# A hybrid layer on one core: attention stacks widened to 128 rows with zero rows, the first sequence's softplus in halves, idle identity products, and three weight loads moved

## Chip, core and metric

The kernel runs on one core of a Trainium2 chip. The metric is the time on the device in microseconds (us); the kernel before took 939.68 us, the median of three runs (939.14 to 942.08).

The core's engines are named as in the profile: PE is TensorE (PEld its weight loads), DVE VectorE, ACT ScalarE, POOL GpSimd, and SP the engine whose queue issues most transfers. A "q" behind an engine's name (SPq, ACTq, POOLq) is that engine issuing a DMA.

## What is computed

The input is x, 4 sequences of 512 tokens with 128 channels. Four blocks follow each other, each added to its input after a layer norm. Cut to the lines that matter here:

```python
x = x + attn_a(layernorm(x))     # rms norm, Mamba block, residual, rms norm, mixture of experts
x = x + ffn(layernorm(x))        # integer weights times 1/127: silu(x Wg) * (x Wu), then Wd
x = x + attn_b(layernorm(x))     # 16 heads of 8, causal softmax, low-rank keys and values
x = x + ffn(layernorm(x))        # the same weights again
# in the Mamba block, for each of 256 inner channels and 16 states:
delta = softplus(dbc[..., :64] @ dt_proj_w + dt_proj_b);  A = -exp(A_log)
h = exp(delta * A) * h + (delta * x) * B;  y = sum over states of h * C
# the mixture of experts: 8 experts, the best 2 for each token
```

## The kernel before, in words

Everything lives in one function, `block_kernel`, in two stages. All line numbers are those of the kernel before.

**Stage 1, the scans (up to about 405 us of the profile).** For each of the 4 sequences, `front` (L707) prepares the Mamba inputs and then 16 steps of `scan` (L860) run, one for each state, over tiles of 128 partitions x 1024 (two groups of 128 channels, 512 tokens each). A step has a fixed shape. ACT makes the decays `da` (L812). PE spreads a row of B over the partitions into `pb` (L822). DVE multiplies `bx = du * pb` (L854) and runs the recurrence `hst` (L874). POOL multiplies `hc = hst * cs` (L886), where `cs` is a row of C that SP fetches (L816) from DRAM, where L769 has put it. PE adds `hc` into `yp` with the identity matrix (L832). The tile `cs` has three buffers, `hst` two, and `bx` one (it fills the PSUM pool `ps_x`).

`front(0)` runs before the first scan, with nothing beside it: layer-norm statistics on DVE, `hn` (L710), a transpose by PE into `hT`, the convolution as 8 products `pm` (L723) with `w_k` as weights, `xi` (L729), the gate `sz` (L740), the scaled residual input `h0` (L743), `pdt` and its copy `dt` (L747, L752), B and C as `pbc` with `bc` and `bc_c` (L757 to L767), and the softplus (L777 to L801): `pd`, |.| and relu of it, exp(-|.|), ln(1 + .), and a correction of what adding 1 rounds off. Its result is `delta`; POOL multiplies it with `xi` to `du` (L803). For sequences 1 to 3 the same generator is drawn out over the steps of the sequence before it, a piece at every `yield`.

Other generators are drawn out beside the scans in the same way, as streams: `close` and `route` of a finished sequence, `scatter` of its tokens to their experts' rows, `experts` (tiles of 128 tokens: two products with 512 columns, a gate, a product back; 256 KB for each of three weight loads), `combine`, `first_ffn`, `project`. One of them is `early` (L661), which runs in the steps of sequence 0. It fills the experts' token buffers `xg` in DRAM with zeros, by 8 transfers of 1 MB on SP's queue (L680), from an SBUF tile with the tag "y". It then loads the three weights of the feed-forward blocks, one after the other, into a tile of the same tag (`raw`, L697), and DVE turns each into float (L693).

**What sets the order.** In stage 1 the order on PE, DVE, ACT and SP is the order of the program text (L34, `manual_schedule`), and each engine and each queue works through it strictly. POOL's multiplication of a step is made to wait for the last small DVE instruction that was drawn into the step (L892). The attention stage has no such order: there the framework's scheduler orders each engine by its own estimate, so that an edit can also move its neighbours.

**Stage 2, attention (to the end).** It works in 8 units of 8 heads. Queries and keys are held as three bf16 parts of their float values, stacked as 72 rows: 9 pairs of parts by 8 dimensions, in tiles `qs` and `ks` of 96 partitions, with 3 buffers each. `fill` (L1079) loads a unit by 6 transfers from DRAM. `maxima` (L1090) multiplies 72 rows of queries with 72 rows of keys (L1104), adds the causal mask by a product with the identity (L1108) and takes row maxima on DVE (L1100). The maxima go back as three more bf16 rows of `qs` (L1133, L1134), against three rows of -1 in `ks` (`below`, L1062). `exps` (L1140) multiplies the 75 rows the other way round (L1157), with a mask again (L1165), and ACT takes the exponential (L1170): 10 tiles for each group of four heads. `weigh` (L1173) multiplies with the values (L1184): four heads side by side, each with 32 columns of the array. Beside these run what is left of the experts' tiles, and the feed-forward blocks and projections of later sequences.

Of the kernel before, what the change touches and what calls it, by code (L numbers as in the profile page):

```python
# [8 lines left out]
F32 = mybir.dt.float32  # L9
# [7 lines left out]
P = 128  # L17
# [20 lines left out]
def block_kernel(ctx, tc, x, rms1_w, rms2_w, in_proj_w, conv_w, conv_b, x_proj_w,  # L38
# [51 lines left out]
    nc.gpsimd.memset(below, -1.0)  # L90
    identb = const.tile([P, P], BF16, tag="identb", name="identb")
# [80 lines left out]
    def transposed(ps, dst, src, scale=None):  # L172

        pt = ps.tile([P, L], F32, tag="mm" if ps is ps_m else "sc", name="pt")
        for t in range(NT):
            nc.tensor.transpose(pt[:, t * P : (t + 1) * P], src[:, t, :], ident)
        if scale is None:
            nc.scalar.copy(dst, pt)
        else:
            nc.scalar.activation(dst, pt, AF.Copy, scale=scale)  # L180
# [416 lines left out]
    with ExitStack() as first:  # L597
# [28 lines left out]
        w_o = load("w_o", [P, C], W_oT)  # L626
        hT = w1.tile([P, L + KW - 1], F32, tag="hT", name="hT")
# [33 lines left out]
        def early():  # L661

            for b in range(2, B):
# [23 lines left out]
            raw = None  # L687
            for dst, src in (
                (fwg, w_gateT), (fwu, w_upT), (fwd, w_downT.rearrange("(c p) m -> p c m", p=P)),
                (None, None),  # L690
            ):
                if raw is not None:
                    nc.vector.tensor_scalar(raw[0], raw[1], 1.0 / 127.0, None, ALU.mult)  # L693
                yield
                if dst is not None:
                    raw = dst, w1.tile(list(dst.shape), I32, tag="y", name="raw")
                    nc.sync.dma_start(raw[1], src)  # L697
# [8 lines left out]

        def front(b):  # L707
# [4 lines left out]
            transposed(ps_s, hT[:, KW - 1 :], hn, r1w[:, 0, :])  # L712
# [22 lines left out]
            for e in range(NE):  # L735
                pm = ps_s.tile([P, L], F32, tag="sc", name="pm")
                nc.tensor.matmul(
                    pm, w_in[:, EI + e * P : EI + (e + 1) * P], hT[:, KW - 1 :], start=True, stop=True
                )
                nc.scalar.activation(sz[b][:, e, :], pm, AF.Silu)  # L740
            yield
            h0[b] = w2.tile([P, NT, C], F32, tag="h0", name=f"h0_{b}")
            scaled(h0[b], xs[b], norms["r"][:, 0, b], norms["m"][:, 0, b])  # L743
            yield "sc"
# [7 lines left out]
            nc.scalar.copy(dt[b], pm[0:DTR, :])  # L752
            yield
# [15 lines left out]
            nc.sync.dma_start(c_d[b], cr[NS : 2 * NS, :])  # L769
            yield  # L770

# [574 lines left out]
```

## Time and profile before

| what | us |
|---|---|
| median of three runs | 939.68 |
| the profiled execution's own time | 941.45 |
| its span, from the first instruction to the last | 939.6 |
| PE busy (share of the span) | 734.1 (78%) |
| DVE busy | 580.3 (62%) |
| ACT busy | 411.2 (44%) |
| POOL busy | 309.4 (33%) |
| first scan step begins (DVE) | 44.61 |
| first attention product begins (PE) | 470.44 |
| mean granted PE clock, share of full speed | 0.854 |

The profile is of one execution; 1.85 us of its own time lie outside its span. "Busy" counts an engine's own instructions. Each view that is shown later gives, for an instruction or a group of instructions: when it starts, how long it takes, the engine, the line, the operation, what it writes from what it reads, and in brackets how long the engine had been idle before and what ended that. PE's records of float products come in pairs, so that one product of 128x512 counts as two. The page cuts the span into 40 slices of 23.5 us; a digit is a share in tenths.

### The profile page before, as it was taken

The page shows a single profiled execution, that of the slowest core. Times are in us where ns is not written, and L with a number is a line of the kernel's source. Part 1 is how long each engine was busy: PE and PEld are TensorE (multiplying, and loading weights), DVE is VectorE, ACT ScalarE, POOL GpSimd, SP SyncE. Part 2 cuts the span into 40 slices and gives each one's busy share as a digit, 9 for nine tenths or more (in the row PEclk, how much of TensorE's full clock was granted, in tenths as well). Part 3 has the DMA queues.
Part 4 walks back from the last instruction along what each step waited for, and adds up shares of the span by engine and source line. Part 5 has one row for each costly group of instructions (what it writes and reads, how often), then busy time and mean ns, then how long its engine had stood idle before and what let it go on. Part 6 is the DMA issues. An engine that isn't in the chain of part 4 may idle for free. (4 is left out here: it accounts for less than half of the span.)

```text
span 939.6 us, 11943 instructions
## 1 busy us (share of the span) xinstructions
PE 734.1 (78%) x3763; PEld 429.0 (46%) x3763; DVE 580.3 (62%) x1151; ACT 411.2 (44%) x794; POOL 309.4 (33%) x243
## 2 busy tenths in 40 slices
PE   5386698689879865788398799789858997889854
PEld 2132243255356621557357476458724454355432
DVE  4395999899989898747274552166544156566311
ACT  2836548535854431324103354503345533554641
POOL 1153664856556348432402104000161402300010
PEclk9688789789989977799759599979968897997987
DMA  4138221163157412516546235817410330600000
GB/s 103 35 140 325 65 68 47 53 194 112 64 171 233 132 46 82 172 46 202 178 125 204 80 117 168 211 45 220 143 43 3 93 87 7 163 16 3 3 12 11
DMA packets 84480, 99.16 MB, mean 106 GB/s; under 512 B 10370, under 2 KB 56458, under 8 KB 83242
## 3 DMA queue, kind: packets, MB, share of 16 engines
q1 hardware_dynamic: 78881, 87.09, 31.3%
q0 software_dynamic: 4352, 10.89, 3.6%
q10 hardware_dynamic: 1184, 0.43, 0.2%
q8 instruction: 30, 0.49, 0.2%
q14 instruction: 33, 0.26, 0.1%
HBM read 76.67 MB, written 21.63 MB: 105 GB/s over the span
## 5 line engine op out<-in xcount | busy, mean ns | idle before, releaser
L886 POOL TENSOR_TENSOR hc<-hst,cs 128x1024 f32<-128x1024 f32 x64 | 150.6, 2353 | 138.7 <-issue 34.3
L832 PE MATMUL yp<-hc,ident 128*128 128x512 f32 x256 | 150.6, 718 | 43.6 <-POOL hc L886 42.5
L874 DVE TENSOR_TENSOR_SCAN hst<-da,bx 128x1024 f32<-128x1024 f32 x64 | 146.3, 2286 | 10.7 <-POOL hc L886 3.7
L1100 DVE TENSOR_REDUCE mx<-sc 128x1 f32<-128x384 f32 (+3 forms) x168 | 102.7, 636 | 66.4 <-PE sc L1108 64.8
L832 PEld LDWEIGHTS yp<-hc,ident 128*128 128x128 f32 x256 | 52.7, 220 | 140.6 <-POOL hc L886 98.9
L1170 ACT ACTIVATE p<-st 128x512 f32<-128x512 f32 x160 | 90.9, 598 | 34.3 <-PE st L1165 31.0
L812 ACT ACTIVATE da<-delta,A 128x512 f32<-128x512 f32 (+1 forms) x128 | 84.7, 715 | 41.1 <-DVE hst L874 38.5
L1104 PE MATMUL sc<-ks,qs 72*128 72x128 bf16 (+3 forms) x256 | 76.7, 358 | 15.5 <-DMA ks<-k_d 8.2
L854 DVE TENSOR_TENSOR bx<-du,pb 128x1024 f32<-128x1024 f32 x64 | 78.3, 1223 | 5.0 <-POOL du L803 2.5
L319 DVE SCALAR_TENSOR_TENSOR thm<-thm,mpg 128x512 f32<-128x512 f32 x53 | 36.1, 680 | 70.4 <-ACT thm L380 70.4
L374 PE MATMUL mpg<-xTm,wgu 128*128 128x128 f32 x424 | 67.1, 301 | 11.1 <-DMA wgu<-in_Wg_dram 6.7
L1157 PE MATMUL st<-qs,ks 75*128 75x512 bf16 (+3 forms) x256 | 67.7, 331 | 10.3 <-ACT p L1170 5.6
L374 PEld LDWEIGHTS mpg<-xTm,wgu 128*128 128x128 f32 x424 | 60.3, 214 | 20.3 <-issue 8.4
L374 PE MATMUL mpu<-xTm,wgu 128*128 128x128 f32 x424 | 62.2, 292 | 5.8 <-DVE mh L320 4.1
L1133 POOL DMA_DIRECT2D m_d<-mT x8 | 4.4, 550 | 184.3 <-ACT mT L1131 184.3
L367 ACT ACTIVATE xTm<-mpt,r2w 128x128 f32<-128x128 f32 x53 | 19.4, 366 | 102.9 <-PE mpt L365 102.9
L386 PE MATMUL mpd<-wd,mh 128*128 128x128 f32 x424 | 60.2, 286 | 2.8 <-ACT xTm L367 2.3
L374 PEld LDWEIGHTS mpu<-xTm,wgu 128*128 128x128 f32 x424 | 57.3, 209 | 8.7 <-DVE mh L320 4.4
L822 PE MATMUL pb<-bc,pick 96*128 96x512 bf16 x64 | 27.4, 429 | 41.8 <-DVE bx L854 38.0
L386 PEld LDWEIGHTS mpd<-wd,mh 128*128 128x128 f32 x424 | 53.4, 197 | 7.0 <-ACT xTm L367 5.3
L1108 PE MATMUL sc<-maskq,identb 128*128 128x128 bf16 (+2 forms) x176 | 50.1, 284 | 0.0
L380 ACT ACTIVATE thm<-mpg 128x512 f32<-128x512 f32 x53 | 31.7, 597 | 40.9 <-PE mpg L374 39.9
(242 smaller groups left out, 1167.1 us busy)
## 6 DMA issues: line engine op xcount, KB each, us to landing
cs<-c_d SPq DMA_DIRECT2D x64, 256.0 KB
wgu<-in_Wg_dram SPq DMA_DIRECT2D x53, 256.0 KB
wgu<-in_Wu_dram SPq DMA_DIRECT2D x53, 256.0 KB
wd<-in_Wd_dram SPq DMA_DIRECT2D x53, 256.0 KB
xg<-zero SPq DMA_DIRECT2D x8, 1024.0 KB
qs<-q_d SPq DMA_DIRECT2D x24, 192.0 KB
k_d<-parts POOLq DMA_DIRECT2D x12, 384.0 KB, 4.0
ks<-k_d SPq DMA_DIRECT2D x24, 192.0 KB
```

Of the source, the lines that this page charges most:

```text
L374: nc.tensor.matmul(pp[:, f, :], w[:, k, f * P : (f + 1) * P], rows_in, start=True, stop=True,)
L386: nc.tensor.matmul(pd, hT[:, f, :], w[:, f, :], start=(f == 0), stop=(f == NFC - 1))
L812: nc.scalar.activation(da[:, e, e:], delta[b][:, e, e:], AF.Exp, scale=A[:, e, n : n + 1])
L832: nc.tensor.matmul(yps[b][:, e, :], ident, hc[:, e, :], start=(n == 0), stop=(n == NS - 1))
L854: nc.vector.tensor_tensor(bxs[s], du[s // NS], taps[s][1].unsqueeze(1).to_broadcast([P, NE, L]), ALU.mult)
L874: nc.vector.tensor_tensor_scan(hst.rearrange("p e l -> p (e l)"), dec.pop(s).rearrange("p e l -> p (e l)"), bxs.pop(s).rearrange("p e l -> ...
L886: done = nc.gpsimd.tensor_tensor(hc, hst, cs.unsqueeze(1).to_broadcast([P, NE, L]), ALU.mult).ins
L1100: nc.vector.tensor_reduce(*taken, AX.X, ALU.max)
L1104: nc.tensor.matmul(sc[:, c : c + w], q[0:NP9, h, t * P : w], k[0:NP9, h, 0:w], start=(h == h0), stop=False, skip_group_check=True,)
L1108: nc.tensor.matmul(sc[:, 0 : n * w].rearrange("p (h k) -> p h k", k=w)[:, :, t * P : w], identb, maskq.unsqueeze(1).to_broadcast([P, n, P] ...
L1157: nc.tensor.matmul(pt[:, c : c + L - kt * P], k[0 : NP9 + 3, h0 + j, rows], q[0 : NP9 + 3, h0 + j, kt * P : L], start=(c == 0), stop=False ...
L1170: ready[G] = nc.scalar.activation(p, pt, AF.Exp, scale=scale).ins
```

## The change

- The tiles of queries and keys have 128 rows. Rows 72 to 124 of both are filled with zeros from a new tile `blank`, by a transfer for each of the six tiles, when `fill` first uses it; the maxima and the rows of -1 go to rows 125 to 127. The products L1104 now run over 125 rows and L1157 over 128. The values of the products stay the same.
- The softplus of sequence 0 is done in two halves of 512 columns. Its relu moves from ACT to DVE, its product `du` from POOL to DVE; exp(A_log) moves from ahead of the convolution to just ahead of the softplus. For sequences 1 to 3 the same steps come in another order, with more `yield`s between them.
- In `front`, `pdt` and its copy come ahead of the gate `sz`. The scaled residual of sequence 0 moves to `early`, so into the first scan step.
- `warm(n)` issues n products of the identity with itself into the buffer of `bx`, whose result nobody reads: 16 at the very start, 1 after each of the 4 transposes of sequence 0, 16 after its `pd`, and 16 after the first `pb`.
- The three feed-forward weights are loaded at the start, behind the other weights on SP's queue, straight into their own tiles, and DVE converts them in place in `early`.

The diff, shortened (`...` for lines left out, blank lines dropped):

```diff
@@ -88,6 +88,9 @@
...
     nc.gpsimd.memset(below, -1.0)
+    blank = const.tile([P - 3 - 9 * HS, L], BF16, tag="blank", name="blank")
+    nc.gpsimd.memset(blank, 0.0)
     identb = const.tile([P, P], BF16, tag="identb", name="identb")
...
@@ -169,11 +172,13 @@
...
-    def transposed(ps, dst, src, scale=None):
+    def transposed(ps, dst, src, scale=None, beside=None):
...
             nc.tensor.transpose(pt[:, t * P : (t + 1) * P], src[:, t, :], ident)
+            if beside:
+                beside()
         if scale is None:
...
@@ -624,6 +629,10 @@
...
         w_o = load("w_o", [P, C], W_oT)
+        for w, raw in (
+            (fwg, w_gateT), (fwu, w_upT), (fwd, w_downT.rearrange("(c p) m -> p c m", p=P))
+        ):
+            nc.sync.dma_start(w.bitcast(I32), raw)
         hT = w1.tile([P, L + KW - 1], F32, tag="hT", name="hT")
...
@@ -660,6 +669,7 @@
...
+            residual(0)
             for b in range(2, B):
...
@@ -684,17 +694,9 @@
...
-            raw = None
-            for dst, src in (
-                (fwg, w_gateT), (fwu, w_upT), (fwd, w_downT.rearrange("(c p) m -> p c m", p=P)),
-                (None, None),
-            ):
-                if raw is not None:
-                    nc.vector.tensor_scalar(raw[0], raw[1], 1.0 / 127.0, None, ALU.mult)
+            for w in (fwg, fwu, fwd):
+                nc.vector.tensor_scalar(w, w.bitcast(I32), 1.0 / 127.0, None, ALU.mult)
                 yield
-                if dst is not None:
-                    raw = dst, w1.tile(list(dst.shape), I32, tag="y", name="raw")
-                    nc.sync.dma_start(raw[1], src)
                 yield
...
@@ -704,12 +706,16 @@
...
+        def residual(b):
+            h0[b] = w2.tile([P, NT, C], F32, tag="h0", name=f"h0_{b}")
+            scaled(h0[b], xs[b], norms["r"][:, 0, b], norms["m"][:, 0, b])
         def front(b):
...
             yield
-            transposed(ps_s, hT[:, KW - 1 :], hn, r1w[:, 0, :])
+            transposed(ps_s, hT[:, KW - 1 :], hn, r1w[:, 0, :], (lambda: warm(1)) if b == 0 else None)
             yield
...
@@ -732,16 +738,6 @@
...
             yield "sc"
-            for e in range(NE):
-                pm = ps_s.tile([P, L], F32, tag="sc", name="pm")
-                nc.tensor.matmul(
-                    pm, w_in[:, EI + e * P : EI + (e + 1) * P], hT[:, KW - 1 :], start=True, stop=True
-                )
-                nc.scalar.activation(sz[b][:, e, :], pm, AF.Silu)
-            yield
-            h0[b] = w2.tile([P, NT, C], F32, tag="h0", name=f"h0_{b}")
-            scaled(h0[b], xs[b], norms["r"][:, 0, b], norms["m"][:, 0, b])
-            yield "sc"
             pm = ps_s.tile([P, L], F32, tag="sc", name="pdt")
...
@@ -750,6 +746,16 @@
...
             nc.scalar.copy(dt[b], pm[0:DTR, :])
+            yield
+            if b:
+                residual(b)
+            yield "sc"
+            for e in range(NE):
+                pm = ps_s.tile([P, L], F32, tag="sc", name="pm")
+                nc.tensor.matmul(
+                    pm, w_in[:, EI + e * P : EI + (e + 1) * P], hT[:, KW - 1 :], start=True, stop=True
+                )
+                nc.scalar.activation(sz[b][:, e, :], pm, AF.Silu)
             yield
...
@@ -767,7 +773,21 @@
...
             nc.sync.dma_start(c_d[b], cr[NS : 2 * NS, :])
-            yield
+            def second():
+                nc.vector.tensor_tensor(rest, cr, bc[b], ALU.subtract)
+                nc.scalar.copy(mid, rest)
+            def third():
+                nc.gpsimd.tensor_copy(bc[b][32:64, :], mid[32:64, :])
+                nc.gpsimd.tensor_tensor(bc[b][64:96, :], rest[64:96, :], mid[64:96, :], ALU.subtract)
+            if b == 0:
+                nc.scalar.activation(A, A, AF.Exp)
+                nc.vector.tensor_scalar(A, A, -1.0, None, ALU.mult)
+            yield
...
@@ -780,24 +800,42 @@
...
                 nc.scalar.activation(y[:, e, :], pd, AF.Abs, bias=dtb[:, e, :])
-                nc.scalar.activation(r[:, e, :], pd, AF.Relu, bias=dtb[:, e, :])
-            yield
-            nc.vector.tensor_tensor(rest, cr, bc[b], ALU.subtract)
-            nc.scalar.copy(mid, rest)
-            yield
-            nc.gpsimd.tensor_copy(bc[b][32:64, :], mid[32:64, :])
-            nc.gpsimd.tensor_tensor(bc[b][64:96, :], rest[64:96, :], mid[64:96, :], ALU.subtract)
+                if b:
+                    nc.scalar.activation(r[:, e, :], pd, AF.Relu, bias=dtb[:, e, :])
+                    continue
+                if e == 0:
+                    second()
+                nc.vector.tensor_scalar(r[:, e, :], pd, dtb[:, e, :], 0.0, ALU.add, ALU.max)
+                nc.scalar.activation(y[:, e, :], y[:, e, :], AF.Exp, scale=-1.0)
+            if b == 0:
+                third()
+                warm(16)
+                for e in range(NE):
+                    nc.scalar.activation(dl[:, e, :], y[:, e, :], AF.Ln, bias=1.0)
+                    nc.vector.tensor_scalar(d[:, e, :], y[:, e, :], 1.0, -1.0, ALU.add, ALU.add)
+                    nc.vector.tensor_tensor(d[:, e, :], d[:, e, :], y[:, e, :], ALU.subtract)
+                    nc.vector.tensor_tensor(r[:, e, :], r[:, e, :], d[:, e, :], ALU.subtract)
+                for e in range(NE):
+                    nc.vector.tensor_tensor(dl[:, e, :], dl[:, e, :], r[:, e, :], ALU.add)
+                for e in range(NE):
+                    nc.vector.tensor_tensor(r[:, e, :], dl[:, e, :], xi[b][:, e, :], ALU.mult)
+                return
+            yield
+            second()
+            yield
+            third()
             nc.scalar.activation(y, y, AF.Exp, scale=-1.0)
             yield
+            nc.scalar.activation(d, y, AF.Identity, bias=1.0)
+            yield
+            yield
+            nc.vector.scalar_tensor_tensor(d, d, -1.0, y, ALU.add, ALU.subtract)
             yield
             nc.scalar.activation(dl, y, AF.Ln, bias=1.0)
-            nc.scalar.activation(d, y, AF.Identity, bias=1.0)
-            yield
-            if b:
-                yield
-                yield
-            nc.vector.scalar_tensor_tensor(d, d, -1.0, y, ALU.add, ALU.subtract)
-            nc.vector.tensor_tensor(dl, dl, d, ALU.subtract)
+            yield
+            nc.vector.tensor_tensor(r, r, d, ALU.subtract)
+            yield
+            yield
             nc.vector.tensor_tensor(dl, dl, r, ALU.add)
...
@@ -864,6 +902,7 @@
...
                 spread(0)
+                warm(16)
                 bxs[0] = ps_x.tile([P, NE, L], F32, tag="bx", name="bx")
...
@@ -987,8 +1026,15 @@
...
+        def warm(n):
+            pw = ps_x.tile([P, NE, L], F32, tag="bx", name="warm")
+            for _ in range(n):
+                nc.tensor.matmul(pw[:, 0, 0:P], ident, ident, start=True, stop=True)
         with tc.manual_schedule(engines=ORDERED):
+            warm(16)
             moments(xs[0], mv0[:, 0])
...
@@ -1010,8 +1056,6 @@
...
             nc.vector.tensor_copy(pick, pick32)
-            nc.scalar.activation(A, A, AF.Exp)
-            nc.vector.tensor_scalar(A, A, -1.0, None, ALU.mult)
             for _ in first:
...
@@ -1052,17 +1096,13 @@
-        NP9 = 9 * HS
+        NP9, MXR = 9 * HS, P - 3
         NU = NH // 2
...
         for i in range(3):
-            qs.append(w1.tile([96, NU, L], BF16, tag=f"qs{i}", name=f"qs{i}"))
-            k = w1.tile([96, NU, L], BF16, tag=f"ks{i}", name=f"ks{i}")
-            nc.sync.dma_start(
-                k[NP9 : NP9 + 3, :, :], below.unsqueeze(1).to_broadcast([3, NU, L])
-            )
-            ks.append(k)
+            qs.append(w1.tile([P, NU, L], BF16, tag=f"qs{i}", name=f"qs{i}"))
+            ks.append(w1.tile([P, NU, L], BF16, tag=f"ks{i}", name=f"ks{i}"))
...
@@ -1080,6 +1120,12 @@
...
             q_d, k_d, _ = stores[b]
+            if u < 3:
+                for stack in (qs[u], ks[u]):
+                    nc.sync.dma_start(
+                        stack[NP9:MXR], blank.unsqueeze(1).to_broadcast([MXR - NP9, NU, L])
+                    )
+                nc.sync.dma_start(ks[u][MXR:P], below.unsqueeze(1).to_broadcast([3, NU, L]))
             for i in range(3):
...
@@ -1102,7 +1148,7 @@
...
                         nc.tensor.matmul(
-                            sc[:, c : c + w], q[0:NP9, h, t * P : w], k[0:NP9, h, 0:w],
+                            sc[:, c : c + w], q[0:MXR, h, t * P : w], k[0:MXR, h, 0:w],
                             start=(h == h0), stop=False, skip_group_check=True,
...
@@ -1131,7 +1177,7 @@
...
             nc.gpsimd.dma_start(m_d.rearrange("i h l -> (i h) l"), mT)
-            nc.gpsimd.dma_start(q[NP9 : NP9 + 3, :, :], m_d)
+            nc.gpsimd.dma_start(q[MXR:P, :, :], m_d)
             yield
...
@@ -1155,8 +1201,8 @@
...
                     nc.tensor.matmul(
-                        pt[:, c : c + L - kt * P], k[0 : NP9 + 3, h0 + j, rows],
-                        q[0 : NP9 + 3, h0 + j, kt * P : L],
+                        pt[:, c : c + L - kt * P], k[:, h0 + j, rows],
+                        q[:, h0 + j, kt * P : L],
                         start=(c == 0), stop=False, skip_group_check=True,
...
                     got[j][kt] = p[:, c : c + L - kt * P]
```

## Prediction

> **What bounds the kernel now.** I began with the page. Its chain of waits that ended last names only the last 120 us, so I cut the span into slices and read where each engine stands idle.
>
> ```profile
> PE   5386698689879865788398799789858997889854
> DVE  4395999899989898747274552166544156566311
> PEclk9688789789989977799759599979968897997987
> DMA  4138221163157412516546235817410330600000
> ```
>
> Slices 5 to 14 (94 to 329 us) belong to DVE at 8 or 9 tenths: the scan steps. Ahead of them DVE has 3 tenths in slice 2 (23 to 47) and 5 in slice 4 (70 to 94). From slice 20 on the end is mostly PE's: 342 busy of the 400 us from 500 to 900 in the table by 20 us, 85%. Its clock digit falls to 5 to 7 in several slices in which PE's own digit stays high.
>
> The time lines of the opening follow, for PE, ACT and DVE. The number behind a start is the time from the first to the last of the merged instructions; a bracket is the idle time before.
>
> ```profile
> 11.80 9.75 PE L723 MATMUL pm<-hT,w_k 128*128 128x512 f32 x16 [0.82 <-issue]
> 21.39 2.06 PE L737 MATMUL pm<-hT,w_in 128*128 128x512 f32 x4
> 23.38 1.93 PE L747 MATMUL pdt<-xi,w_xp 128*64 128x512 f32 x4
> ```
>
> ```profile
> 23.98 1.64 ACT L167 ACTIVATE h<-x,m,r 128x128 f32<-128x128 f32 x4
> 25.52 0.57 ACT L752 COPY dt<-pdt 64x512 f32<-64x512 f32 x1
> 36.98 1.28 ACT L812 ACT_TABLE_LOAD   x1
> 40.78 3.78 ACT L812 ACTIVATE da<-delta,A 128x512 f32<-128x512 f32 x6 [2.51 <-DVE delta L801]
> ```
>
> ```profile
> 37.00 1.23 DVE L799 SCALAR_TENSOR_TENSOR sp_d<-sp_d,sp_y 128x1024 f32<-128x1024 f32 x1 [7.97 <-ACT sp_d L794]
> 43.28 1.23 DVE L854 TENSOR_TENSOR bx<-du,pb 128x1024 f32<-128x1024 f32 x1 [2.53 <-POOL du L803]
> 44.61 2.29 DVE L874 TENSOR_TENSOR_SCAN hst<-da,bx 128x1024 f32<-128x1024 f32 x1
> ```
>
> Until 44.61 the kernel is one chain of dependent work, so whatever leaves this chain shortens the kernel. Next, DVE's time line from 75 to 106, with SP's queue:
>
> ```profile
> 78.93 2.29 DVE L874 TENSOR_TENSOR_SCAN hst<-da,bx 128x1024 f32<-128x1024 f32 x1
> 90.87 0.36 DVE L693 TENSOR_SCALAR fwg<-raw 128x384 f32<-128x384 int32 x1 [9.65 <-DMA raw<-in_w_gateT_dram]
> 92.50 2.29 DVE L874 TENSOR_TENSOR_SCAN hst<-da,bx 128x1024 f32<-128x1024 f32 x1
> ```
>
> ```profile
> 77.93 1.34 SPq L816 DMA_DIRECT2D cs<-c_d  x1
> 88.40 0.34 SPq L697 DMA_DIRECT2D raw<-in_w_gateT_dram  x1
> ```
>
> The load of `raw` waits until the zero transfers have read the tile whose place it takes (88.40). DVE, which works in program order, stands before the conversion for 9.65 us, with the next step's `bx` behind it. Last, the table by stretches for attention: length, busy time of PE, PEld, DVE, ACT and POOL, then the granted clock.
>
> ```profile
> 525.70:536.00 10.30, 10.30 (x46) 5.95 (x44) 5.82 (x19) 7.15 (x14) 0.00 (x0) 0.50 0.15 53
> 856.80:866.10 9.30, 9.24 (x41) 4.90 (x38) 5.95 (x16) 5.89 (x11) 1.13 (x1) 0.50 0.01 2
> 870.50:877.40 6.90, 5.87 (x45) 3.25 (x41) 3.65 (x10) 6.74 (x15) 0.52 (x1) 1.00 0.00 1
> 594.00:597.40 3.40, 3.35 (x16) 3.38 (x17) 0.64 (x1) 0.60 (x1) 0.00 (x0) 0.50 0.75 156
> ```
>
> In the first two, PE is full and still has half its clock. The third is a like group of ten score tiles at full clock, bound by ACT.
>
> **Part 1, the opening.** The first eight records of L723 follow each other at 0.85 us, the last eight at 0.43: the clock opened at about 17.1. The 16 idle products can begin when `ident` stands, at about 1.6 us. At half clock each takes 0.43, so they fill PE until the clock opens within 6.9 us (one to two of the 3.4 us windows in which the clock changes in this trace); those between the transposes bridge to 11.8. Then L723 takes 16 x 0.43 = 6.9 us and ends at 18.7, not 21.55. The clock being closed again by 11.8 would cost 2.9.
>
> - `pdt` now follows at once, its second half at 19.5 after `xi`, and ends at 20.4. `dt` ends at 21.0, not 26.09: the gate's products (2.06) and `h0` (1.64) stood before it. They cover ACT's and PE's gaps now; `h0` goes into scan step 0, whose decays are needed only two steps later. That is nothing.
> - PE: gate to 22.1, `pbc` to 23.9, `pd` to 25.8. ACT: `bc_c` ends at 25.0, table 1.28, exp of A 0.22, then |.|, `bc_mid`, exp, |.|, exp in pieces of 0.6 to 0.69 to 29.6; table 1.28 to 30.9; two logarithms to 32.0; table to 33.3, and the decays of step 0 to 34.7.
> - DVE: ten pieces of 512 columns at 0.65 (half of 1.22, plus overhead; `bc_rest` with 512 took 0.69). POOL's two copies of `third` run to 29.5; beside POOL the conversion `fwd` (L693) took 1.20 against 0.36, so I let DVE's first correction wait until 29.5. Six corrections to 33.5, two sums and two products to 36.0, `bx` 1.23, scan at about 36.4: **8.2 us earlier** than 44.61.
> - The 16 idle products after the first `pb` (30.0 to 33.4 at full clock) hold the buffer of `bx` and must end before 36. With a closed clock they end at 36.8 and cost about 1. The 16 after `pd` run while PE waits for POOL. The zero tile is one more POOL memset (`below` took 0.51) in POOL's idle start.
>
> **Part 2, the weights ahead of zeros.** Three issues of about 0.4 us more on SP at 14 us, and 576 KB when the DMA row stands near zero (16 to 28 us): nothing; the next on that queue is `c_d`, at 25. The conversions stay, at 0.36. What is late next is `cs`, in the same queue behind the zeros. The row for the step at 78.93 was issued at 73.15, behind six zero transfers and five rows (7.5 MB at the 0.39 MB/us of 64 to 80 us), so it lands at about 83; the two after it at about 89. On these times POOL's three products run at 83.5, 89 and 91.4, and DVE's steps at 82.9, 86.9 and 91.7 where before they stood at 92.50, 97.03 and 101.71: **10 us**. If `cs` lands with the last zeros at 88.4, the gain is 3.
>
> **Part 3, softplus of sequences 1 to 3.** The same DVE work, spread over three steps instead of one. DVE bounds these steps, so I count 0. `sp_d` at 187.36 took 3.68 beside POOL's product instead of 1.2, which spreading can remove or repeat: -2 to +2 for each of three, kept for the range.
>
> **Part 4, 128 rows.** [...] The fourth row, all of 128-row products, opened at 597.4 after one window. If I add up the columns of all products in a window at the granted clock, each weighted by its rows over 128, the windows of the first two are 0.63 to 0.72 full, and those after which the clock opened are at 0.75 and more. I take the trace: the clock counts rows. With 128 rows:
>
> - 856.8 to 870.5 (13.7 us) becomes like the group after it (6.9, plus 2.4 for L1184, less overlap): -4.8.
> - 525.7 to 538: one window to open, then 8.9 us become 5.5: -3.4.
> - 682.7 to 689.6: -3. 723.7 to 737.3: -4.5 if the clock stays open at 723.7, taken at 3/4: -3.4.
> - Stretches of maxima alone (474 to 487, 621 to 628, 771 to 778) run at DVE's 0.73 us for each L1100, clock or not: 0. The experts' products behind two of them (4.7 and 6.5 us at half clock) may gain 5, half counted: -2.4.
>
> That is 17. PE holds the end for some 85% of this stage and ACT, DVE or a transfer is next otherwise, so I take 13 of it. Against it stand six zero fills of 434 KB on SP's queue, ahead of unit loads and the experts' weights. From 460 to 480 us transfers with such packets moved 208 GB/s at a share of 0.79, so a fill is 1.7 us, 10 in all. The queue is half idle there: I count 1, bounds 0 and 10. The scheduler also reorders PE in units 0 and 1: +-3. Net **-12**.
>
> **Sum.** 941.45 - 8.2 - 10 - 12 = 911.3 us for the profiled execution. The median lies 1.8 below it: **909.5 us**.
>
> **Rivals.**
>
> [...]
> - *The head gives less*: the clock closes before 11.8 (2.9) and `cs` takes the place of `raw` (7): 909.5 + 7 to 10 = 918. For it speaks that `cs` queues behind zeros already at 77.88.
> - *PE holds the end everywhere*, and fewer closings also spare experts and feed-forward products: 25 in part 4, so 897.
> - *The zero fills decide*, and the kernel is slower: they stand in SP's queue ahead of the loads of units 1 and 2 and of experts' weights. All six would have to delay PE in full, and to cost more than 5 us each instead of 1.7. At 6 us: 909.5 + 36 = 945.
> - *Nothing measurable*: the fills eat the gain, at 5 us each.
>
> **Chances.** Likeliest case 0.60 (own range 901 to 917), no clock gain 0.13, smaller head 0.11, larger gain 0.09, no change 0.02, slower 0.05. About 0.3% (2.8 us) is what a measurement can tell from no change. So faster has 0.93, same 0.02, slower 0.05. The range reaches 897 to 925.
>
> **What would show it.** First scan at 36 to 37 us; L723 at 0.43 a record from the start (if not, the clock closed). Scan step 11 (101.71 before) starting about 47 us after step 0 instead of 57.1, with no DVE wait of 9 us among them. In attention, granted clock 1.00 in stretches where PE is full for over 3.4 us; if they stay at 0.50, part 4 is wrong. A PE wait on `ks<-k_d` or `wgu` of over 5 us behind a zero fill would make the slower rival right.

## The result

The changed kernel is slower: 974.52 us, the median of four runs (972.95 to 977.13), against 940.88 us for the kernel before, run beside it (939.14 to 942.87). The ratio is 1.036, with a 95% interval from 1.032 to 1.040. The forecast was 909.5 us with a range from 897 to 925. The profiled execution took 972.95 us, its span is 971.2.

Line numbers from here on are those of the changed kernel, unless another one is named. The four rows of the page that answer to those shown of before, in slices of 24.3 us:

```profile
PE   8797795898889568645439962988975897889864
DVE  4899998999897978414144650218554437547511
PEclk9798998899998659867678885999997997979987
DMA  4175211632672135044446413583630050320000
```

The head is better: DVE is at 7 to 9 tenths in slices 2 to 16, PE at 8 in the first. The last third has PE mostly at 7 to 9, with a clock of 7 to 9. What is lost lies between. PE falls to 4, 5, 4 and 3 in slices 18 to 21 and to 2 in slice 25, where DVE has 0 and the DMA row 3. So in 583 to 607 us the kernel waits for transfers while most of the DMA engines are idle. PE's time line shows that wait, and SP's shows what stood in the queue:

```profile
600.57 2.05 PE L379 MATMUL mpg<-xTm,wgu 128*128 128x128 f32 x8 [27.29 <-DMA wgu<-in_Wg_dram]
```

```profile
386.25 14.66 SPq L1125 DMA_DIRECT2D ks<-blank  x1
400.96 18.09 SPq L1128 DMA_DIRECT2D ks<-below  x1
...
559.25 14.35 SPq L350 DMA_DIRECT2D yg<-ym  x1
...
576.16 0.71 SPq L1125 DMA_DIRECT2D ks<-blank  x1
576.92 16.01 SPq L1128 DMA_DIRECT2D ks<-below  x1
593.17 0.35 SPq L362 DMA_DIRECT2D wgu<-in_Wg_dram  x1
```

The second column is how long the issue took, 0.3 to 1 us for most. The issue behind each of the six zero fills takes 14 to 18 us: 14.66 behind the first, of queries, at 385.32, and 18.09 behind the second. From 559 on SP is held for 14.35 us (behind a fill at 558.36) and again for 16.01, and the experts' weights `wgu`, for which PE waits 27.29 us, come only behind both. The table by stretches, of 412 to 418, while the second fill drains (its bytes move):

```profile
412.00:418.00 6.00, 0.00 (x0) 0.00 (x0) 0.00 (x0) 0.00 (x0) 0.00 (x0) 0.50 0.07 24
```

The last two columns are the DMA share and GB/s. 0.07 is about one of sixteen engines, and 434 KB at 24 to 27 GB/s are 16 to 18 us, the time for which SP's queue stands. The list of waits has the sum for `wgu` in us, the times and the longest, of before and then of now:

```profile
PE mpg L374 <- DMA wgu<-in_Wg_dram: 6.7, 4, 4.4
```

```profile
PE mpg L379 <- DMA wgu<-in_Wg_dram: 60.0, 11, 27.3
```

PE now waits 60.0 us for `wgu`, and the list puts 13.7 us more down to `wd`, the third of the experts' weights.

The opening and the weights, on PE's time line and then on DVE's:

```profile
1.55 6.70 PE L1033 MATMUL warm<-ident 128*128 128x128 f32 x32 [1.55 <-POOL ident masks.py:199]
...
11.97 7.11 PE L729 MATMUL pm<-hT,w_k 128*128 128x512 f32 x16 [0.39 <-issue]
```

```profile
29.88 0.75 DVE L808 TENSOR_SCALAR du<-pd,dtb 128x512 f32<-128x512 f32 x1 [1.13 <-ACT sp_y L802]
...
38.12 2.29 DVE L913 TENSOR_TENSOR_SCAN hst<-da,bx 128x1024 f32<-128x1024 f32 x1
...
74.74 0.34 DVE L698 TENSOR_SCALAR fwu<-fwu 128x384 f32<-128x384 int32 x1
...
85.39 2.29 DVE L913 TENSOR_TENSOR_SCAN hst<-da,bx 128x1024 f32<-128x1024 f32 x1 [0.20 <-POOL hc L925]
```

The convolution takes 7.11 us instead of 9.75, ACT has `dt` ready at 21.56 where the forecast had 21.0, and the first scan step starts at 38.12 instead of 44.61: 6.5 us won. The conversions cost 0.34 with no wait ahead of them, and step 11 starts at 85.39, 47.3 us after step 0 (57.1 before). These two parts came as forecast, or nearly.

### The profile page after: what moved, and what is told of

Its sections match the earlier page's. It is cut to its first block, busy times and chain, and to the rows that moved or that the text cites. A ratio compares the mean times of both kernels' runs of the same rounds, so it can differ in the third digit from the quotient of the medians.

```text
span 971.2 us, 12151 instructions
## 1 busy us (share of the span) xinstructions
PE 723.3 (74%) x3858; PEld 436.2 (45%) x3867; DVE 582.2 (60%) x1160; ACT 408.7 (42%) x793; POOL 308.6 (32%) x243
## 5 line engine op out<-in xcount | busy, mean ns | idle before, releaser
L870 PE MATMUL yp<-hc,ident 128*128 128x512 f32 x256 | 148.4, 709 | 47.4 <-POOL hc L925 46.1
L1150 PE MATMUL sc<-ks,qs 125*128 125x128 bf16 (+3 forms) x256 | 66.1, 316 | 29.5 <-DMA wd<-in_Wd_dram 13.7
L1203 PE MATMUL st<-qs,ks 128*128 128x128 bf16 (+3 forms) x247 | 59.0, 300 | 12.4 <-ACT p L1216 6.8
L391 PE MATMUL mpd<-wd,mh 128*128 128x128 f32 x424 | 62.6, 290 | 2.2 <-ACT xTm L372 1.3
L391 PEld LDWEIGHTS mpd<-wd,mh 128*128 128x128 f32 x424 | 55.4, 202 | 7.2 <-ACT xTm L372 3.9
L263 POOL DMA_INDIRECT xg<-hs,rows x32 | 32.4, 1012 | 45.8 <-DVE rows L255 38.4
L1154 PE MATMUL sc<-maskq,identb 128*128 128x128 bf16 (+2 forms) x176 | 45.4, 258 | 0.0
```

The source lines that it names most:

```text
L391: nc.tensor.matmul(pd, hT[:, f, :], w[:, f, :], start=(f == 0), stop=(f == NFC - 1))
L870: nc.tensor.matmul(yps[b][:, e, :], ident, hc[:, e, :], start=(n == 0), stop=(n == NS - 1))
L1150: nc.tensor.matmul(sc[:, c : c + w], q[0:MXR, h, t * P : w], k[0:MXR, h, 0:w], start=(h == h0), stop=False, skip_group_check=True,)
L1154: nc.tensor.matmul(sc[:, 0 : n * w].rearrange("p (h k) -> p h k", k=w)[:, :, t * P : w], identb, maskq.unsqueeze(1).to_broadcast([P, n, P] ...
L1203: nc.tensor.matmul(pt[:, c : c + L - kt * P], k[:, h0 + j, rows], q[:, h0 + j, kt * P : L], start=(c == 0), stop=False, skip_group_check=True,
```

## The experiments

Theory 1: the six zero fills are the whole loss; all else won what it should, or more. Theory 2: some other part of the change costs the 65 us between forecast and measurement. Theory 3: zero rows do nothing for the clock. Within theory 1 it is open why a fill is so slow: 1a, its 53 rows; 1b, its size, its 1 KB pieces, or its single source. The ratios below are to the kernel before on the same chip, whose median was 938.5, 937.4 and 940.3 us in the three groups of four.

**The stacks as before** (opening, weights and softplus as changed):

```diff
...
-            qs.append(w1.tile([P, NU, L], BF16, tag=f"qs{i}", name=f"qs{i}"))
-            ks.append(w1.tile([P, NU, L], BF16, tag=f"ks{i}", name=f"ks{i}"))
+            qs.append(w1.tile([96, NU, L], BF16, tag=f"qs{i}", name=f"qs{i}"))
+            k = w1.tile([96, NU, L], BF16, tag=f"ks{i}", name=f"ks{i}")
+            nc.sync.dma_start(
+                k[NP9 : NP9 + 3, :, :], below.unsqueeze(1).to_broadcast([3, NU, L])
+            )
+            ks.append(k)
...
```

> The changed kernel with the stacks of before: 72 and 75 rows, no zero rows and no zero fills; opening and weights as changed. Theory 1 (the six zero fills are what made it slower; opening and weights brought what the changed profile shows, 6.5 us to the first scan and 9.8 us in steps 0 to 11): 940.9 - 16.3 = about 924.5 us, 919 to 929. Theory 2 (something else of the change costs the 60 us that are missing: the weights early, the softplus spread over steps, or the warm products): it stays above 941. The attention stage should look like before's, with PE full at a granted clock of 0.50 in some stretches.

Measured: 920.51 us, ratio 0.980 (0.976 to 0.985). Theory 2 falls: without the 128 rows the change is a gain of 18 us.

**Zeros by POOL instead of by transfers:**

```diff
                 for stack in (qs[u], ks[u]):
-                    nc.sync.dma_start(
-                        stack[NP9:MXR], blank.unsqueeze(1).to_broadcast([MXR - NP9, NU, L])
-                    )
+                    nc.gpsimd.memset(stack.bitcast(F32)[P // 2 : P], 0.0)
```

> The changed kernel, but the zero rows are written by POOL (rows 64 to 127 of a stack as 64 x 2048 float words of zero, ahead of the loads that fill rows 64 to 71) instead of by the six transfers. Theory 1 (the transfers were the loss, and the clock counts rows): the head's 16.3 us stay and the clock's 12 to 13 come on top, 911 us, 904 to 917; no PE wait for wgu above 7 us. Theory 3 (transfers were the loss, but zero rows do nothing for the clock): 922 to 927, as with the old stacks. Theory 2 (something else): above 941.

Measured: 903.23 us, ratio 0.962 (0.959 to 0.966). Only how the zeros get there has changed, and some 70 us are gone. Theory 1 holds, and the time is just below its 904 to 917. Theory 3's 922 to 927 are missed by far.

**Fills of 56 rows instead of 53:**

```diff
-    blank = const.tile([P - 3 - 9 * HS, L], BF16, tag="blank", name="blank")
+    blank = const.tile([P - 9 * HS, L], BF16, tag="blank", name="blank")
...
-                        stack[NP9:MXR], blank.unsqueeze(1).to_broadcast([MXR - NP9, NU, L])
+                        stack[NP9:P], blank.unsqueeze(1).to_broadcast([P - NP9, NU, L])
```

> The changed kernel with one number changed: a zero fill has 56 rows (72 to 127) instead of 53, and the rows of -1 overwrite the last three afterwards. The changed profile shows a DMA share of 0.07 to 0.08 and 23 to 27 GB/s while a fill of 53 rows drains, which is what one of 16 engines gives. Theory 1a (the 53 rows cannot be dealt out over the engines, 56 can, by 8 or 14): a fill takes 1.5 to 3 us, SP's queue stands 0 to 2 us instead of 14 to 18, and the time is near that of zeros written by POOL, 912 to 920. Theory 1b (the fill is slow for its size, its 1 KB pieces or because all rows read the same tile): a fill takes 17 us and the time is 972 to 980.

Measured: 898.04 us, ratio 0.957 (0.953 to 0.961), below the 912 to 920 expected. Three rows more per fill, and the kernel is 40 us faster than before instead of 34 slower. Each read against its own runs of before, 1.036 against 0.957, the difference is 0.079, or 74 us, 12 for each fill. The longest of SP's issues around the fills, the stretch in which these drain, and two of the page's rows:

```profile
388.76 1.75 SPq L1125 DMA_DIRECT2D qs<-blank  x1
```

```profile
391.00:394.00 3.00, 2.98 (x19) 2.46 (x20) 0.69 (x1) 0.03 (x1) 0.12 (x1) 1.00 0.91 179
```

```profile
PE   7797697699889865788478898888948988799854
...
PEclk9899899799999966899789899999969997889977
```

The same 1 KB pieces from the same source now move at 179 GB/s and a share of 0.91 instead of 24 and 0.07. At that rate a fill of 459 KB takes 2.6 us, and PE waits 3.3 us in all for `wgu`. Theory 1b falls: the row count alone made the fills slow.

**Only the 128 rows, on the kernel before** (zeros by POOL; opening, weights and softplus as before), and its **control**, with the same tiles and zeros but the products over 72 and 75 rows:

```diff
+                    nc.gpsimd.memset(stack.bitcast(F32)[P // 2 : P], 0.0)
...
-                            sc[:, c : c + w], q[0:NP9, h, t * P : w], k[0:NP9, h, 0:w],
+                            sc[:, c : c + w], q[0:MXR, h, t * P : w], k[0:MXR, h, 0:w],
```

> The kernel before with nothing but the 128 rows, zeros written by POOL: opening, weights and softplus as before. Theory of the prediction (the clock counts rows): 940.9 - 12 = 929 us, 924 to 934, with a granted clock of 1.00 in stretches where PE is full. Rival (the clock follows how busy PE is, whatever the rows): 940 to 943, and PE full at 0.50 for over 7 us somewhere.

> The kernel before with stacks of 128 partitions and the zeros written by POOL, but the products still over 72 and 75 rows and the rows of -1 at 72 to 74: everything of the run with only the 128 rows but the rows themselves. Theory (its 17 us come from the rows that the clock counts): 938 to 942, PE full at a granted clock of 0.50 in the stretches where it was so before. Rival (they come from the other tiles, the memsets and the order that the scheduler then chooses): 920 to 930.

Measured: 921.38 us with the rows, ratio 0.982 (0.977 to 0.986); 937.54 us for the control, ratio 0.997 (0.993 to 1.001). So the rows themselves bring about 17 us. The table by stretches, of the kernel with the rows in a place that answers to 525.7 of before, then of the control in one that answers to 856.8:

```profile
526.30:536.60 10.30, 10.21 (x81) 5.83 (x80) 5.83 (x19) 8.54 (x18) 0.00 (x0) 1.00 0.18 53
```

```profile
855.70:865.90 10.20, 10.20 (x45) 5.26 (x46) 6.63 (x20) 6.25 (x11) 1.22 (x1) 0.50 0.01 2
```

With the rows the granted clock (third number from the end) is 1.00, and the stretch holds 81 products (46 before). The control stays at 0.50 with PE full for all 10.2 us, and gets 45 done.

I counted this over the whole second part of the traces. In these traces the clock changes only at the edges of a grid of 3.41 us. I took every window of that grid after 380 us in which the clock stood at 0.50 and PE was busy for 0.85 or more, and looked whether the next window was granted 1.00. Kernels with 72 or 75 rows: 19 of 34 (before), 17 of 31 (old stacks), 13 of 30 (control) and 15 of 27 (only the weights, further down) were not. With 128 rows: none of 13 (only the rows), of 10 (zeros by POOL) and of 9 (56 rows), and 8 of 70 in the six others. Weighted by rows over 128, with heads side by side counted once, the windows not followed by 1.00 hold at most 0.74 of full work in all runs, the others at least 0.71. Three of those eight are in the changed kernel. The table by stretches for two that follow each other, and one line of PE's time line in that stretch:

```profile
529.80:536.60 6.80, 6.49 (x25) 5.54 (x26) 1.64 (x3) 0.67 (x2) 4.33 (x5) 0.50 0.83 243
```

```profile
532.12 1.22 PE L1111 MATMUL pv<-veff,qk 64*128 64x128 f32 x4
```

PE is busy for 6.49 of 6.8 us and the clock stands at 0.50. The values' products `pv` there, 2.4 of the 6.5 us, were left at 64 rows.

**96 rows, on the kernel before:**

```diff
-        NP9, MXR = 9 * HS, P - 3
+        NP9, ROWS9 = 9 * HS, 96
+        MXR = ROWS9 - 3
...
-                    nc.gpsimd.memset(stack.bitcast(F32)[P // 2 : P], 0.0)
+                    nc.gpsimd.memset(stack.bitcast(F32)[P // 2 : ROWS9], 0.0)
```

> The kernel before with 96 rows in the products instead of 72, 75 or 128, zeros written by POOL. Theory (the clock counts columns weighted by rows, and opens at about 0.75 of a window): windows full of products of queries and keys rise from 0.67 to about 0.81 and open, as from 525.7 and 856.8 on, those that were 0.48 to 0.57 for their gaps rise to 0.6 and stay closed; some 8 to 12 of the 17 us, 927 to 932. Rival (any zero row, or none, makes the difference): 921 or 940.

Measured: 933.05 us (19 runs, 926.8 to 940.0), ratio 0.997 (0.994 to 0.999). The gain is below what I expected: 3 to 4 us (1 to 6 by the interval), not 8 to 12. Ten of 27 windows with PE full stayed closed, with a row-weighted share of at most 0.69. The direction fits, but I had set too high what 96 rows would open.

**Fills of several sizes** (54 and 55 rows for unit 0; 52 and 1, and 56, for unit 1; 51 and 2, and 53, for unit 2):

```diff
-                for stack in (qs[u], ks[u]):
-                    nc.sync.dma_start(
-                        stack[NP9:MXR], blank.unsqueeze(1).to_broadcast([MXR - NP9, NU, L])
-                    )
+                for stack, n in zip((qs[u], ks[u]), ((54, 55), (52, 56), (51, 53))[u]):
+                    for lo, hi in ((NP9, NP9 + n), (NP9 + n, MXR)):
+                        if hi > lo:
+                            nc.sync.dma_start(
+                                stack[lo:hi], blank[0 : hi - lo].unsqueeze(1).to_broadcast([hi - lo, NU, L])
+                            )
```

> The changed kernel with six fills of different sizes: 54 rows for the queries and 55 for the keys of unit 0, 52 and 1 for the queries and 56 for the keys of unit 1, 51 and 2 for the queries and 53 for the keys of unit 2. A look at the DMA share and GB/s while each drains. Theory 1a' (a transfer is dealt to as many engines as the largest number up to 16 that divides its rows): 54 to 9 engines, 55 to 11, 52 to 13, 56 to 14, shares of 0.5 to 0.9 and 2 to 4 us each; 51 to 3 engines, 0.19 and 5 us; 53 to one, 0.06 and 16 us. Rival (only rows that are a multiple of 4 or 8 are dealt out): 54, 55, 51 and 53 all at one to two engines, 0.06 to 0.13 and 8 us or more. In all: with one slow fill left of 53 rows and one of 51, 900 to 918 us under 1a', above 930 under the rival.

Measured: 917.98 us, one run. The table by stretches, of 51 rows and then of 53:

```profile
513.00:514.60 1.60, 1.60 (x6) 0.74 (x5) 0.55 (x1) 0.82 (x2) 0.00 (x0) 1.00 0.19 52
530.00:532.00 2.00, 0.00 (x0) 0.00 (x0) 0.00 (x0) 0.69 (x2) 0.00 (x0) 1.00 0.08 27
```

Shares of 0.19 and 0.08 are about 3 and 1 of 16 engines, and 53 rows again stop PE and DVE. The trace's records of single packets say the same: three are under way at a time for 51 rows, one for 53, and 14 for the 56 rows of the run above, from 391 to 394. While the 54 and 55 rows drain, from 388 to 390, the share is 0.71, at 152 GB/s. So the traces agree with theory 1a' for 53, 51 and 56 rows. What it says of 54, 55 and 52 is not shown: these fills overlapped in the queue, so their single numbers are not told apart. The rival falls with the 0.71 and the 0.19: it had 0.13 at most for each of 54, 55 and 51 rows.

**Each fill of 53 cut into 52 and 1:**

```diff
+                    for lo, hi in ((NP9, MXR - 1), (MXR - 1, MXR)):
+                        nc.sync.dma_start(
+                            stack[lo:hi], blank[0 : hi - lo].unsqueeze(1).to_broadcast([hi - lo, NU, L])
+                        )
```

> The changed kernel with each fill of 53 rows cut into one of 52 and one of 1 row, the rows of -1 as in the change. Theory 1a' (dealt to the largest number up to 16 that divides the rows: 52 to 13 engines, the one row, 8 KB, to one): a fill takes some 2.6 us, SP stands less than 4 us at each, and the time is that of 56 rows, 896 to 902. Rival (the last row alone drains as slowly as the 53 did): above 930.

Measured: 899.06 us, ratio 0.958 (0.951 to 0.965), as with 56 rows, though it issues six transfers more. So it is not the amount that is slow, and the one row left over does no harm.

**Without the idle products** (fills of 56 rows): every `warm` call is left out.

> The changed kernel with fills of 56 rows and without any of the idle identity products. Prediction's step (they save the time of a closed clock at the convolution): L723 takes 9.75 us instead of 7.1, the first scan step starts 2.6 to 3.5 us later, the time is 898 + 3 = 901. Rival (the clock would open anyway, or the products cost as much as they save): 897 to 899.

Measured: 898.55 us, ratio 0.955 (0.949 to 0.961), against 898.04 with them: no difference, as the rival had it. PE's time line of the kernel without them, then of the one with fills of 56 rows:

```profile
11.48 9.38 PE L729 MATMUL pm<-hT,w_k 128*128 128x512 f32 x16 [0.82 <-issue]
```

```profile
12.13 8.53 PE L729 MATMUL pm<-hT,w_k 128*128 128x512 f32 x16 [0.37 <-issue]
```

The first scan step starts at 39.89 without and at 39.70 with the products, but at 38.12 in the changed kernel, whose opening has the same code. The 16 first products end at 6.91 with fills of 56 rows and at 8.25 in the changed kernel: where the grid of 3.41 us lies differs from run to run. In the changed kernel the clock opened at 7.6, in the run with 56 rows at 4.8, but there the window from 8.2 to 11.6 held only the transposes and the single products between them, and at its end the clock closed again. Seven traces have this opening. In five the convolution took 7.11 us and the first scan began at 38.1 to 38.2; in two, of 56 rows and of POOL's zeros, it took 8.4 to 8.5 and the scan began at 39.5 to 39.7. So the same products are worth 1.7 to 1.8 us or 0.2 to 0.4.

**More idle products** (fills of 56 rows, 20 and 2 products, A's sign changed later):

```diff
-            transposed(ps_s, hT[:, KW - 1 :], hn, r1w[:, 0, :], (lambda: warm(1)) if b == 0 else None)
+            transposed(ps_s, hT[:, KW - 1 :], hn, r1w[:, 0, :], (lambda: warm(2)) if b == 0 else None)
...
-            warm(16)
+            warm(20)
             moments(xs[0], mv0[:, 0])
...
```

> The changed kernel with fills of 56 rows, 20 instead of 16 products at the start and 2 instead of 1 after each transpose, and the change of A's sign behind the relus on DVE. Theory (with fills of 56 rows the clock, open early, closed again in the thin stretch of the transposes; twice the products keep it open): L723 takes 7.1 to 7.3 us instead of 8.1 and the first scan step starts at 37.8 to 38.3 instead of 39.7; in time 1.5 us, less than can be told apart, 895 to 899. Rival (the products delay the transposes): L723 starts 0.5 us or more later and nothing is gained.

Measured: 899.36 us, ratio 0.957 (0.950 to 0.964).

Parts of both expectations came true: the clock was open, with 7.11 us for the convolution, and the products delayed its start by 0.5 us, to 12.60. The first scan step starts at 38.45, just outside the 37.8 to 38.3. As five of seven traces with fewer products were open too, this one trace does not show that the added ones kept the clock open, and in the time nothing can be told.

**Only the weights ahead of the zeros, on the kernel before:**

```diff
+        for w, raw in (
+            (fwg, w_gateT), (fwu, w_upT), (fwd, w_downT.rearrange("(c p) m -> p c m", p=P))
+        ):
+            nc.sync.dma_start(w.bitcast(I32), raw)
...
```

> The kernel before with nothing but the three weight loads put ahead of the zeros, conversions in place. Prediction's step: scan step 11 starts 47 us after step 0 instead of 57.1, no DVE wait for raw, and the time is 10 us less, 928 to 930. Rival (the wait goes into the row cs, which stands in the same queue behind the zeros): 3 us less, 935 to 937, with a POOL wait for cs of 5 us or more in these steps.

Measured: 924.45 us, ratio 0.984 (0.978 to 0.991). In the trace step 11 starts at 91.47, 47.4 us after step 0 at 44.06, and POOL waits 5.5 us for `cs` in all, 3.6 at most (3.9 and 2.2 before), so the rival's wait is there in part, but not its loss. The scans end 9.5 us earlier (step 63 at 386.65, not 396.17). The measured gain, 9 to 21 us, holds the 10 of the forecast. The profiled execution gained 18: behind the scans it is 8 to 9 us shorter too, for which no cause was looked for.

**The old softplus order for sequences 1 to 3** (fills of 56 rows; the three corrections of DVE back in one step):

```diff
...
             nc.vector.scalar_tensor_tensor(d, d, -1.0, y, ALU.add, ALU.subtract)
-            yield
-            nc.scalar.activation(dl, y, AF.Ln, bias=1.0)
-            yield
-            nc.vector.tensor_tensor(r, r, d, ALU.subtract)
-            yield
-            yield
+            nc.vector.tensor_tensor(dl, dl, d, ALU.subtract)
             nc.vector.tensor_tensor(dl, dl, r, ALU.add)
```

> The changed kernel with fills of 56 rows, and the softplus of sequences 1 to 3 as before (relu subtracted last, both corrections of DVE in one step). Prediction's step: nothing, within 6 us either way of 898, most likely 896 to 901. Rival (spreading the corrections over steps is where some of the gain beyond the forecast comes from): 904 to 910.

Measured: 905.7 us (902.3 to 910.0), ratio 0.964 (0.958 to 0.970), beside 899.1 (894.5 to 905.8) for the new order in the same group (the kernel with 52 and 1 rows): inside the rival's 904 to 910, but the ranges of the two touch. DVE's time line of the old order, then of the new one, both from a step that starts at 170.79:

```profile
176.71 1.23 DVE L836 TENSOR_TENSOR delta<-delta,sp_d 128x1024 f32<-128x1024 f32 x1
177.97 1.22 DVE L837 TENSOR_TENSOR delta<-delta,du 128x1024 f32<-128x1024 f32 x1
```

```profile
176.59 1.22 DVE L892 TENSOR_TENSOR bx<-du,pb 128x1024 f32<-128x1024 f32 x1
```

Ahead of these lines the first correction of the step, at 173.0, is stretched to 3.68 us in both. In the old order two more follow in the same step, in the new one the next step's `bx` goes on at once. Four steps later the old order is at 196.07 and the new one at 192.42, and at the end of the scans (step 63) at 382.84 and 375.13. Against the order of before, without the other edits, the difference is smaller: from step 0 to step 63 the weights alone give 342.6 us, the whole new head 336.9 to 339.3, so 3 to 6 us for all that the head changes besides.

## Why the prediction was wrong, step by step

- **The zero fills (the step that failed).** "From 460 to 480 us transfers with such packets moved 208 GB/s at a share of 0.79, so a fill is 1.7 us, 10 in all. The queue is half idle there: I count 1, bounds 0 and 10." A fill drained in 16 to 18 us, SP's queue stood for 14 to 18 us behind each, and PE waited for the weights behind them: 12 us of the kernel's time for each fill, 74 in all, where the sum had 1. The 1.7 us stand for all sixteen engines (208 over 0.79 is 263 GB/s). The row was the wrong one. None of its packets has the fills' 1 KB: apart from single words, the trace's records have 512 bytes to 16 KB there, of the experts' weights and tokens and of queries and keys. And the number of rows was not looked at. Two nearer rows stood in the trace of before: the three transfers of 3 rows, `ks<-below`, that drain from 408 to 410 with little beside them, and the loads of queries and keys, 24 rows each, that drain alone from 466 to 470.

```profile
408.00:410.00 2.00, 0.17 (x1) 0.17 (x1) 0.81 (x2) 0.00 (x0) 1.78 (x1) 0.92 0.15 26
466.00:470.00 4.00, 0.00 (x0) 0.00 (x0) 0.00 (x0) 0.00 (x0) 0.00 (x0) 0.50 0.72 172
```

A share of 0.15 for 3 rows and of 0.72 for 24 (3 and 12 sixteenths are 0.19 and 0.75) already say that these transfers did not reach all engines. That 53 rows would reach only one, neither row shows. For that case an estimate from the row of 24 rows: 172 GB/s over 12 engines are 14 for one, and 434 KB take 30 us. The fills took 16 to 18, at 24 to 27 GB/s.
- **The rival "the zero fills decide".** Its mechanism and its place were right: the wait on `wgu` behind a fill is there. Its price was set at 6 us, and its chance at 0.05. With 12 us for each fill it gives 909.5 + 72 = 981.5, which is 7 above the 974.5 measured, as the other parts brought some 10 more than the sum had. As all six fills have the same 53 rows, "all six" was no unlikely condition.
- **The opening, 8.2.** 6.5 in the changed kernel. Two terms were mis-sized. The steps themselves (corrections to 36.0, then `bx` 1.23) give 37.2 and not 36.4. And the corrections began at 30.55, not 29.5, because DVE's second relu stood ahead of them until ACT was done with |.|. The identity products are no firm part of it: 4 to 5 us come from the rest of the new opening (39.89 without any product, 44.0 to 44.7 in the kernels with the old one), and 0.2 to 1.8 from the clock. The stretch that should "bridge to 11.8" bridged in five traces and failed in two.
- **The weights, 10.** Right: 9.7 us by step 11, and `cs` did not take the place of `raw`.
- **The softplus of sequences 1 to 3, 0.** Too low, as far as the touching ranges tell. Against the old order in the new head, spreading won 5 to 8 us, 3.7 of it in the preparation of sequence 2, and not because it removed the stretched instruction, as the range allowed for: that stayed at 3.68.
- **The 128 rows, 13 before the fills.** Right in the mechanism, and low in size. Busy time alone does not decide whether the clock opens: 19 of 34 windows with PE full stayed closed before, none of 13 with the rows. Alone, with POOL's zeros, the rows brought 17 us (13 to 21). That this is the sum of the stretches before the discount for what is late next may be luck, as the stretches were not measured one by one. With the new head and fills of 56 rows they brought 22 (0.957 against the 0.980 of the old stacks; the intervals of the two gains overlap), nearer to the 25 of the rival in which PE holds the end everywhere. The table by parts, from the end of the scans on, of the kernel before and of the one with 52 and 1 rows:

```profile
397.00:940.00 543.00, 439.68 (x2787) 282.23 (x2786) 256.84 (x680) 211.44 (x436) 97.22 (x104) 0.85 0.34 95
```

```profile
376.20:893.00 516.80, 409.45 (x2783) 267.27 (x2781) 253.91 (x680) 210.02 (x435) 97.10 (x104) 0.92 0.37 104
```

PE does the same products in 409 us instead of 440, at a clock of 0.92 instead of 0.85, and the part is 26 us shorter, so most of the 30 that PE won is kept. The old stacks with the new head give 541.1 us and 0.84 for this part. With the rows and POOL's zeros it is 522.5 on the old head and 523.9 on the new one: 6 to 7 us more than with quick fills, which is about the difference between 17 and 22. Why is open, as the control, with the same zeros, has 542.7, no more than before.
- **The sum.** With the fills mended (52 and 1 rows) the span goes from 939.6 to 893.3 us: 21 ahead of the end of the scans, where the sum had 18.2, and 26 behind it, where it had 12. The medians, 898 to 899 us, are those of the rival with the larger gain (897).

## What to carry to other kernels

Before a transfer is costed, look at the number of its rows, not only at its bytes and its packets: here a fill of 53 rows kept about one of sixteen engines busy (a share of 0.07), one of 51 about three (0.19) and one of 56 fourteen (0.91), and SP's queue stood for 14 to 18 us behind each fill of 53, with the experts' weights waiting in it. Three rows more (56 for 53), or a row cut off (52 and 1), cost nothing and was worth 74 us here. When PE is full and its clock stays low, count the rows of its products: zero rows up to 128 took no time of their own (a product of 512 columns has a median of 380 ns with 75 rows and of 379 with 128) and opened the clock here (19 of 34 full windows stayed at 0.50 before, none of 13 with only the rows added), while products put in only to keep it awake brought nothing that the time could show (898.04 us with them, 898.55 without).

## What the runs showed of the hardware that I had not expected

- A fill's rate changed with its row count, with the same packets and source: 53 rows moved 24 to 27 GB/s, 51 rows 52, 56 rows 179. Theory 1a' agrees with the 1, 3 and 14 engines of these three, and with some 12 (0.72 of sixteen) for the loads of 24 rows before; no run shows it alone for 52, 54 or 55.
- SP's next issue took 14.4 to 18.1 us behind a fill of 53 rows in the changed kernel, and 13.3 in the run with several sizes, but 1.7 us behind that run's fill of 51, which drained for 5 us more. What sets how long the queue stands was not tried.
- The clock's grid of 3.41 us lies differently from run to run against the kernel's start, so that the same identity products opened the clock for the convolution in the changed kernel (at 7.6; 7.11 us), while with fills of 56 rows it opened at 4.8 and closed again (8.53).
- Six memsets of POOL (1.8 us each, 64 x 2048 words) cost more than quick fills: 903.2 us against 898.0 with 56 rows. Why was not tried.
